# Layer 0 of a four-layer graph network: two half-height row blocks at the start, x loaded first, a wider V tile, a matmul spread of the first row terms, and the layernorm applied on GpSimd

## The chip, the cores and the metric

The kernel is one program on one core of a Trainium2 chip. The metric is the device time of one execution in microseconds, lower is better. A core has five engines with an instruction queue each, and each queue runs in order: TensorE (matmul, PE in the profile, with PEld for its weight loads), VectorE (DVE), ScalarE (ACT), GpSimd (POOL) and SyncE (SP, which here only starts DMA transfers). Transfers are also started from the ACT and POOL queues; an instruction that starts one occupies its queue until it is issued.

## What is computed

Four layers, each `x = x + layer(relu(layernorm(x)), adj)`, on x of 4096 x 256 (float32) with an adjacency matrix of 4096 x 4096 (int32, under 1% ones). Layer 0 is the one that the change works on. Of its reference, this part matters here:

```
h = relu(layernorm(x))
Wh = h @ W                                     # 4096 x 256
e = Wh @ a_src + (Wh @ a_dst).T                # one row term, one column term
e = where(e > 0, e, 0.2 * e)
attn = softmax(where(adj > 0, e, -9e15), axis=1)
h_attn = attn @ Wh                             # the attention of layer 0
...                                            # a dense part on Wh and h_attn follows, then
x = x + layernorm(gate * h_attn + ...)
```

Layer 1 averages neighbours, layer 2 is an attention of the same kind as layer 0's (slope 0.01, its own W and a), layer 3 is a dot-product attention. They use the adjacency matrix too, in the transposed and coded form that layer 0 leaves in DRAM (`codesT`).

## The kernel before

**Tiles.** N is 4096, so there are NT = 32 row tiles of 128 rows. `xs` holds all of x in SBUF. Layer 0's attention takes RB = 4 row tiles at a time: NRB = 8 blocks. Inside a block it goes over the 32 column tiles in pairs, PPB = 16 pairs for each block, 128 pairs in all.

**Attention, one pair** (class `Attention`, `run`, line 272). For a pair of column tiles VectorE makes `y` (L265, two instructions, 128x512 each: four row tiles by one column tile) from `ab_row`, the row terms of the block spread over all partitions; GpSimd subtracts the mask codes (L269, 128x1024); ScalarE takes the exponential (L295, two of 128x512); TensorE multiplies into four accumulators (L306): two column tiles by four row tiles, and each float32 matmul stands in the trace as two instructions, so 16 for a pair. The right operand is `v`, which has the 256 columns of Wh and a column of ones, from which the softmax's denominator comes. The matmuls of a pair come LAG = 3 pairs behind its `y`; `y` has 8 buffers. When a block is done, `finish0` scales the accumulators into `xs`.

**Row terms** (`reach`, line 215). Before a block can begin, its row maxima must be known: `run` is a running minimum over all 32 column tiles of code minus column term (L227 and L229, one instruction for each column tile), LEAD = 3 pairs ahead of one block. Then `run` is copied out of PSUM (L235), transposed (L238), reduced (L241), combined with the source terms in four small instructions (L242 to L246), transposed again (L248), copied (L250), written to DRAM (L251) and read back into all partitions (L253).

**Adjacency codes** (`fresh`, line 345). A unit is one row tile by 1024 columns of `adj`, 128 units in all. A GpSimd DMA loads it and casts it to bfloat16 (L351, tile `adj_t`, 8 buffers), TensorE transposes it in eight matmuls (L354) into one PSUM tile `cT`, ScalarE turns it into codes in `turned` (L358). `turned` tiles hold four row tiles by 1024 columns, and there are 8 of them. Each is also written to `codesT` (L368, 1 MB). In the main loop `ahead(n)` makes one unit for each pair, UPB + FRESH = 24 units ahead of the pair.

**Prologue** (`block0`, line 377; `run_staggered`, eight blocks of four row tiles). Each block makes three units, loads its x (L382, SP queue), takes layernorm statistics on VectorE (L121, L122), adds epsilon (L114), raises to -0.5 on GpSimd (L116), computes an offset (L131), applies scale, offset and relu on ScalarE (L133, four of 128x256), transposes on TensorE (L144, eight matmuls), copies the two results out on VectorE and ScalarE (L109, L107), multiplies by `w2` (L150, `project`; sixteen instructions of 128x258), copies the two term columns into `sd` on VectorE (L208) and the 256 columns into `v` on ScalarE (L209), and runs `reach` for two pairs. `w2` is W with two columns `W @ a_src` and `W @ a_dst` (`weights`; W and a come over the POOL queue, L181 and L188). After the eighth block `reach` is run through the rest and three pairs of the next block.

**Other loads.** The small weights of the dense part (`bcw`, `bcb`, built in lines 397 to 425) are started on the ACT queue and combined on VectorE. `identb`, the bfloat16 identity that the adjacency transposes need, is cast on VectorE (L67).

**Order.** The engines' queues are not filled in the order of the text: a scheduler at build time takes instructions as it expects them to become ready and hoists loads as far as buffers allow. Thus the casts and copies of a later part can stand ahead of earlier work in an engine's queue, and the queue then waits for them.

Of the kernel before, what the change touches and what calls it, by code (L numbers as in the profile page):

```python
# [11 lines left out]
F32 = mybir.dt.float32  # L12
# [9 lines left out]
P = 128  # L22
# [19 lines left out]
def kernel(ctx: ExitStack, tc: tile.TileContext, w: dict, out: bass.AP):  # L42
# [24 lines left out]
    nc.vector.tensor_copy(identb, ident)  # L67
# [70 lines left out]
    def transposed_block(work, pst, h, tag):  # L138

        hT = work.tile([P, KD, BW], F32, tag=tag, name=tag)  # L140
        for k in range(KD):
            ps = pst.tile([P, BW], F32, tag="tp", name="tp")
            for i in range(BT):
                nc.tensor.transpose(ps[:, ts(i, P)], h[:, i, ts(k, P)], ident)  # L144
            evac(k, hT[:, k, :], ps)
        return hT
# [12 lines left out]

    class Attention:  # L160
        def __init__(self, outer, es, tag, slope, lag, n_y, turned, finish):
            self.tag, self.slope, self.lag, self.n_y = tag, slope, lag, n_y
            self.turned, self.finish = turned, finish
            vp = outer.enter_context(tc.tile_pool(name=f"{tag}_v", bufs=1))
            self.v = vp.tile([P, NT, D + 1], F32, name="v")
            nc.gpsimd.memset(self.v[:, :, D : D + 1], 1.0)
            vp = es.enter_context(tc.tile_pool(name=f"{tag}_sd", bufs=1))
            self.sd = vp.tile([P, NT, 2], F32, name="sd")
            self.sdst = vp.tile([P, NT], F32, name="sdst")
            self.cdst = vp.tile([P, NT], F32, name="cdst")  # L170
            self.ab_d = dram.tile([NRB, 2, RB, P], F32, name=f"{tag}_ab_d")
# [4 lines left out]
            self.blocks = [{} for _ in range(NRB)]  # L176

        def weights(self, wp, work, wm, a_srcs):

            w2 = wp.tile([P, KD, D + 2], F32, name="w2")  # L180
            nc.gpsimd.dma_start(  # L181
# [4 lines left out]
            for a in a_srcs:  # L186
                n = a.shape[0]
                nc.gpsimd.dma_start(  # L188
# [11 lines left out]
            self.w2 = w2  # L200
        def project(self, b, hT, psm):

            sd = self.sd
            for i in range(BT):
                t = b * BT + i
                ps = psm.tile([P, D + 2], F32, tag="mm", name="mm")
                products(ps, lambda k: hT[:, k, ts(i, P)], lambda k: self.w2[:, k, :], KD)
                nc.vector.tensor_copy(sd[:, t, :], ps[:, D : D + 2])  # L208
                nc.scalar.copy(self.v[:, t, 0:D], ps[:, 0:D])  # L209
            at = ts(b, BT)  # L210
            nc.vector.tensor_scalar(self.sdst[:, at], sd[:, at, 1], self.slope, None, ALU.mult)
            nc.vector.tensor_scalar(
                self.cdst[:, at], sd[:, at, 1], 1.0 - self.slope, None, ALU.mult
            )

        def reach(self, n):
# [4 lines left out]
            st = self.blocks[b]  # L221
            if c == 0:
                st["run"] = self.ps_run.tile([P, RB, P], F32, tag="run", name="run")
            for j in range(c, c + 2):
                code = self.turned(b, j // QT)[:, :, j % QT, :]
                if j == 0:
                    nc.vector.tensor_scalar(st["run"], code, self.sd[:, j, 1:2], None, ALU.subtract)  # L227
                else:
                    nc.vector.scalar_tensor_tensor(  # L229
                        st["run"], code, self.sd[:, j, 1:2], st["run"], ALU.subtract, ALU.min  # L230
# [3 lines left out]
            run = self.row_p.tile([P, RB, P], F32, tag="run", name="run_sb", bufs=1)  # L234
            nc.scalar.copy(run, st["run"])  # L235
            ps = self.ps_top.tile([P, RB, P], F32, tag="top", name="top")
            for r in range(RB):
                nc.tensor.transpose(ps[:, r, :], run[:, r, :], ident)  # L238
            src = self.sd[:, ts(b, RB), 0]
            m = self.small.tile([P, RB], F32, tag="m", name="m")  # L240
# [3 lines left out]
            ab = self.small.tile([P, 2, RB], F32, tag="ab", name="ab")  # L244
            nc.vector.tensor_tensor(ab[:, 0, :], src, m, ALU.subtract)
            nc.vector.scalar_tensor_tensor(ab[:, 1, :], src, self.slope, m, ALU.mult, ALU.subtract)  # L246
            ps = self.ps_top.tile([2 * RB, P], F32, tag="top", name="abT")
            nc.tensor.transpose(ps, ab.rearrange("p v r -> p (v r)"), ident)  # L248
            abT = self.small.tile([2 * RB, P], F32, tag="abT", name="abT_sb")
            nc.scalar.copy(abT, ps)  # L250
            nc.sync.dma_start(out=self.ab_d[b].rearrange("v r i -> (v r) i"), in_=abT)  # L251
            st["ab"] = self.row_p.tile([P, 2, RB, P], F32, tag="ab", name="ab_row")
# [5 lines left out]
        def logits(self, y, b, c, mask):  # L258

            st = self.blocks[b]  # L260
            if c == 0:
                st["b"] = self.ps_b.tile([P, RB, P], F32, tag="b", name="b")
# [765 lines left out]
```

## Time and profile before

| | us |
|---|---|
| median of 3 runs | 3092.32 (3087.59 to 3093.89) |
| profiled execution, its own time | 3085.67 |
| its span, first to last instruction | 3083.9 |
| first matmul of layer 0's attention (L306) | 114.90 |
| first matmul of its second block | 180.43 |
| last matmul of its eighth block | 630.36 |
| layer 2: last matmul of layer 1 to first of its attention | 1555.13 to 1631.18 |

Over the whole span TensorE is busy 2869.8 us (93%), VectorE 1851.4 (60%), ScalarE 1271.7 (41%), GpSimd 873.3 (28%). The page's second part, in 40 equal slices of 77 us, shows where TensorE is not full: digits 5 and 7 in the first two slices, a 6 in the slice from 1234 us, a 7 in the one from 1542 us, and 9 elsewhere. The granted TensorE clock is 0.976 on average. How to read it: the share of the span is an average; the first two slices hold the prologue of layer 0 and the start of its attention, and each stage has its own limit.

### The profile page before, as it was taken

What the parts mean: (1) busy time and instruction counts of PE and PEld (TensorE: products, weight loads), DVE (VectorE), ACT (ScalarE), POOL (GpSimd) and SP (SyncE); (2) the same over time, 40 slices, a digit from 0 to 9 for tenths busy, and PEclk for the clock granted to TensorE, in tenths of its full rate; (3) what the DMA queues carried; (4) which work ended last, traced back from release to release, by engine and by line L of the source; (5) the groups of instructions that cost most, each with busy time, mean ns of one, the idle gap of its engine ahead of it and who ended that gap; (6) DMA issues with size and microseconds to landing.
All of it is one profiled execution on the core that took longest, in us unless ns stands there. A gap on an engine that the chain in (4) does not pass through costs nothing.

```text
span 3083.9 us, 34813 instructions
## 1 busy us (share of the span) xinstructions
PE 2869.8 (93%) x13344; PEld 2336.0 (76%) x13344; DVE 1851.4 (60%) x3306; ACT 1271.7 (41%) x1924; POOL 873.3 (28%) x605
## 2 busy tenths in 40 slices
PE   5799999979999999699977999999999999999999
PEld 4688888845555555588856888788888888888888
DVE  5767676324444444544479888755856656656653
ACT  5655655358888884400044443444211211211211
POOL 3556665532333233100016555661000000000000
PEclk9899999989999999899998999999999999999999
DMA  8666664054444341234322222202111111111100
GB/s 209 144 132 136 126 139 110 7 178 129 142 129 132 122 132 40 87 110 147 99 103 82 76 77 81 76 7 69 57 38 37 58 37 37 58 37 37 56 8 7
DMA packets 103127, 268.75 MB, mean 87 GB/s; under 512 B 10704, under 2 KB 24272, under 8 KB 94768
## 3 DMA queue, kind: packets, MB, share of 16 engines
q1 hardware_dynamic: 79104, 220.30, 21.4%
q0 software_dynamic: 22464, 45.51, 8.7%
q8 instruction: 104, 1.70, 0.2%
q10 hardware_dynamic: 1392, 0.72, 0.1%
q14 instruction: 63, 0.52, 0.1%
HBM read 262.22 MB, written 37.81 MB: 97 GB/s over the span
## 4 chain that ended last, share of the span: by engine, by line
PE 27%; issue 25%; DVE 3%; POOL 2%; DMA 1%; ACT 1%; POOLq 0%; DVEq 0%; ACTq 0%
PE acc L306 12%; PE acc L723 8%; PE s L150 3%; PE mm L150 2%; PE acc L960 2%; DVE run L229 1%; POOL y L269 1%; DMA turned<-codesT 1%; DVE y L265 1%; POOL pl_rs L116 1%; POOL out_dram L973 1%; DVE pl_st L121 0%; ACT y L295 0%; DVE hT L109 0%; PE tp L144 0%
## 5 line engine op out<-in xcount | busy, mean ns | idle before, releaser
L306 PE MATMUL acc<-v,y 128*128 128x257 f32 x4096 | 927.1, 385 | 42.5 <-ACT y L295 19.9
L306 PEld LDWEIGHTS acc<-v,y 128*128 128x128 f32 x4096 | 774.4, 192 | 158.1 <-ACT hp L754 22.7
L269 POOL TENSOR_TENSOR y<-y,turned 128x1024 f32<-128x1024 f32 x256 | 547.1, 2150 | 307.7 <-DVE y L265 267.5
L295 ACT ACTIVATE y<-y,sdst 128x512 f32<-128x512 f32 x512 | 342.9, 714 | 367.7 <-POOL y L269 367.5
L265 DVE SCALAR_TENSOR_TENSOR y<-ab_row,cdst,b 128x512 f32<-128x512 f32 x512 | 362.1, 743 | 180.2 <-PE acc L306 115.8
L960 PE MATMUL acc<-v,y 128*128 128x257 f32 x2048 | 454.5, 380 | 0.4 <-DVE rden L968 0.4
L150 PE MATMUL s<-qT,hT 128*128 128x256 f32 x2048 | 445.2, 379 | 0.7 <-ACT qT L908 0.7
L150 PEld LDWEIGHTS s<-qT,hT 128*128 128x128 f32 x2048 | 389.0, 190 | 54.2 <-ACT qT L908 1.4
L960 PEld LDWEIGHTS acc<-v,y 128*128 128x128 f32 x2048 | 387.1, 190 | 55.9 <-issue 0.8
L953 ACT ACTIVATE y<-y 128x1024 f32<-128x1024 f32 x128 | 132.2, 1055 | 714.3 <-DVE y L952 710.0
L229 DVE SCALAR_TENSOR_TENSOR run<-turned,sd,run 128x512 f32<-128x512 bf16 x496 | 373.4, 753 | 49.8 <-DMA turned<-codesT 28.3
L513 ACT ACTIVATE sign<-a,limits 128x1024 bf16<-128x1024 int32 x256 | 293.8, 1148 | 79.6 <-DMA a<-in_adj_dram 75.0
L973 POOL DMA_DIRECT2D out_dram<-o x32 | 17.4, 543 | 933.7 <-DVE rden L968 931.1
L723 PE MATMUL acc<-v,eq 128*128 128x512 f32 x1024 | 239.3, 395 | 0.1
L922 DVE SCALAR_TENSOR_TENSOR y<-code,s 128x512 f32<-128x512 bf16 x256 | 175.8, 687 | 100.5 <-PE s L150 100.2
L723 PEld LDWEIGHTS acc<-v,eq 128*128 128x128 f32 x1024 | 192.6, 188 | 44.9 <-DVE eq L719 0.3
L952 DVE TENSOR_TENSOR y<-y,top 128x1024 f32<-128x1024 f32 x128 | 146.2, 1216 | 43.0 <-PE top L946 43.0
L929 DVE TENSOR_TENSOR mx<-mx,y 128x512 f32<-128x512 f32 x224 | 154.8, 691 | 7.4
L358 ACT ACTIVATE turned<-cT,log_wide 128x1024 bf16<-128x1024 bf16 x128 | 141.5, 1106 | 33.5 <-PE cT L354 33.2
L719 DVE TENSOR_SCALAR eq<-code 128x4096 fp32r<-128x4096 bf16 x32 | 73.4, 2293 | 114.8 <-PE acc L723 114.8
L150 PE MATMUL mm<-hsT,w_L_gnn_W_hz 128*128 128x512 f32 x256 | 117.4, 598 | 0.6 <-DVE hsT L576 0.6
L354 PE MATMUL cT<-identb,adj_t 128*128 128x128 bf16 x1024 | 83.2, 226 | 36.4 <-DVE identb L67 18.5
(222 smaller groups left out, 2717.3 us busy)
## 6 DMA issues: line engine op xcount, KB each, us to landing
a<-in_adj_dram SPq DMA_DIRECT2D x128, 512.0 KB, 3.8
adj_t<-in_adj_dram POOLq DMA_DIRECT2D x128, 256.0 KB, 4.5
codesT<-turned SPq DMA_DIRECT2D x32, 1024.0 KB, 5.1
code<-codesT SPq DMA_DIRECT2D x128, 256.0 KB, 3.8
turned<-codesT SPq DMA_DIRECT2D x32, 1024.0 KB, 5.4
code<-codesT SPq DMA_DIRECT2D x64, 512.0 KB, 4.9
ab_row<-l_ab_d SPq DMA_DIRECT2D x16, 512.0 KB, 3.9
xs<-in_x_dram SPq DMA_DIRECT2D x8, 512.0 KB, 11.0
```

What stands on the lines that cost most here:

```text
L150: nc.tensor.matmul(out=ps, lhsT=lhsT_of(k), rhs=rhs_of(k), start=(k == 0), stop=(k == n - 1))
L229: nc.vector.scalar_tensor_tensor(st["run"], code, self.sd[:, j, 1:2], st["run"], ALU.subtract, ALU.min)
L265: nc.vector.scalar_tensor_tensor(y[:, :, k, :], st["ab"][:, 0, :, :], self.cdst[:, c + k : c + k + 1], st["b"], ALU.add, ALU.max,)
L269: nc.gpsimd.tensor_tensor(y, y, mask[:, :, c % QT : c % QT + 2, :], ALU.subtract)
L295: nc.scalar.activation(y[:, :, k, :], y[:, :, k, :], AF.Exp, bias=self.sdst[:, c + k : c + k + 1],)
L306: nc.tensor.matmul(out=accs[b][r], lhsT=y[:, r, k, :], rhs=self.v[:, c + k, :], start=(c + k == 0), stop=(c + k == NT - 1),)
L513: nc.scalar.activation(sign, a, AF.Sign, bias=limits[:, v : v + 1], accum_out=over[:, t, v, q : q + 1],)
L723: nc.tensor.matmul(out=acc, lhsT=eq[:, ts(c, P)], rhs=v1[:, c, :, :], start=(c == 0), stop=(c == NT - 1),)
L922: nc.vector.scalar_tensor_tensor(y[:, :, c : c + 2, :], st["code"][:, :, c : c + 2, :], -BIG / UNIT, ps, ALU.mult, ALU.add,)
L929: nc.vector.tensor_tensor(mx, mx, y[:, :, c : c + 2, :], ALU.max)
L952: nc.vector.tensor_tensor(part, part, top, ALU.subtract)
L960: nc.tensor.matmul(out=accs[r], lhsT=st["y"][:, r, c, :], rhs=v3[:, c, :], start=(c == 0), stop=(c == NT - 1),)
```

## The change

It has eight parts, all around the prologue of layer 0 except the second, which layer 2 shares.

1. The eight row blocks of layer 0 become nine: `cuts = [(0, 2), (2, 2), (4, 4), ...]`. The first two have two row tiles each, and share the four `turned` tiles of the first four rows. `Attention` takes the list, and every tile of a block is cut to its height.
2. `v` becomes 259 columns: ones first, then Wh, then the source and column terms. One ScalarE copy of 128x258 replaces the VectorE copy into `sd` and the ScalarE copy of 256 columns, in layers 0 and 2.
3. For block 0 the row terms don't go through DRAM: four matmuls with a selecting matrix `picks` spread them into PSUM, and ScalarE and VectorE copy them out.
4. x is loaded ahead of the block loop, blocks alternating between the SP and ACT queues; W, a_src and a_dst of layer 0 go over the ACT queue.
5. Subtraction of the mean and scaling are done on GpSimd (four of 128x256 with two operations each), and the relu goes into the copy out of the transposes, now both on ScalarE. The offset instruction is gone.
6. Units are made by need: in the prologue block b has made b + 1 units, and 1, 2, 3, 5, 7, 9, 11, 13 are loaded; eight more buffers (`first_p`) take the first eight. In the main loop `needed(n)` counts the units of the pair 24 pairs ahead.
7. The dense part's small weights are loaded on the SP queue two pairs into the last block, and combined on VectorE eight pairs into it.
8. `identb` is cast on GpSimd.

```diff
-    nc.vector.tensor_copy(identb, ident)
+    nc.gpsimd.tensor_copy(identb, ident)
...
-    def transposed_block(work, pst, h, tag):
+    def transposed_block(work, pst, h, tag, relu=False):
...
-            evac(k, hT[:, k, :], ps)
+            if relu:
+                nc.scalar.activation(hT[:, k, :], ps, AF.Relu)
+            else:
+                evac(k, hT[:, k, :], ps)
...
-            self.v = vp.tile([P, NT, D + 1], F32, name="v")
-            nc.gpsimd.memset(self.v[:, :, D : D + 1], 1.0)
+            self.v = vp.tile([P, NT, D + 3], F32, name="v")
+            nc.gpsimd.memset(self.v[:, :, 0:1], 1.0)
...
-                nc.vector.tensor_copy(sd[:, t, :], ps[:, D : D + 2])
-                nc.scalar.copy(self.v[:, t, 0:D], ps[:, 0:D])
+                nc.scalar.copy(self.v[:, b * BT + i, 1 : D + 3], ps)
...
+            if self.picks is not None and b == 0:
+                ps = self.ps_top.tile([P, 2 * n, P], F32, tag="top", name="spread")
+                for k in range(2 * n):
+                    nc.tensor.matmul(
+                        out=ps[:, k, :], lhsT=self.picks[:, k, :], rhs=abT, start=True, stop=True
+                    )
+                for v in range(2):
+                    evac(1 - v, st["ab"][:, v, :, :], ps[:, ts(v, n), :])
+                return
...
+            cuts = [(0, 2), (2, 2)] + [(t, RB) for t in range(RB, NT, RB)]
...
+            units = [
+                (at // RB, q, r % RB)
+                for at, n in cuts for q in range(NQ) for r in range(at, at + n)
+            ]
...
+            def load(up_to):
+                for b, q, r in units[len(raw) : up_to]:
+                    pool = first_p if len(raw) < FIRST else adj_p
+                    raw.append(pool.tile([P, QW], BF16, tag="adj", name="adj_t"))
+                    nc.gpsimd.dma_start(out=raw[-1], in_=adj[ts(b * RB + r, P), ts(q, QW)])
...
+            def needed(n):
+                b, c = n // PPB, n % PPB
+                if b >= len(cuts):
+                    return len(units)
+                return cuts[b][0] * NQ + cuts[b][1] * NQ * (c + 1) // PPB
...
             def ahead(n):
-                if n + UPB + FRESH < NRB * UPB:
-                    fresh(n + UPB + FRESH)
+                fresh(needed(n + PPB + FRESH))
...
+                for b in range(NB):
+                    (nc.scalar if b % 2 else nc.sync).dma_start(
+                        out=xs[:, ts(b, BT), :],
+                        in_=x[ts(b, BW), :].rearrange("(t p) d -> p t d", p=P),
+                    )
...
-                    preln(small, xb, xb)
+                    mv = small.tile([P, BT, 2], F32, tag="pl_mv", name="pl_mv")
+                    for i in range(BT):
+                        stats_of(small, xb[:, i, :], mv[:, i, :], "pl")
+                    rs = rstd_of(small, mv, BT, "pl")
+                    load(b + 1 + max(b - 2, 0))
+                    for i in range(BT):
+                        nc.gpsimd.tensor_scalar(
+                            xb[:, i, :], xb[:, i, :], mv[:, i, 0:1], rs[:, i : i + 1],
+                            ALU.subtract, ALU.mult,
+                        )
+                    fresh(b + 1)
                     yield
-                    hT = transposed_block(work, pst, xb, "hT")
+                    hT = transposed_block(work, pst, xb, "hT", relu=True)
                     yield
                     att.project(b, hT, psm)
                     yield
-                    for n in range(2 * b, 2 * b + 2 if b < NB - 1 else PPB + LEAD):
+                    for n in range(2 * b, 2 * b + 2):
                         att.reach(n)
 
                 run_staggered([block0(b) for b in range(NB)], 2)
...
+                fresh(needed(PPB + FRESH - 1))
+                for n in range(PPB, PPB + LEAD):
+                    att.reach(n)
```

## The prediction, made before the changed kernel ran

> **What bounds the kernel now.** I read the page's slices first, then busy time by stage (microseconds from the start, then busy time and count of each engine, granted clock, DMA share, GB/s):
>
> ```profile
> 0.00:48.00 48.00, 17.65 (x96) 13.95 (x97) 23.23 (x114) 16.83 (x28) 18.14 (x37) 1.00 0.81 200
> 48.00:90.00 42.00, 36.62 (x297) 31.46 (x297) 27.64 (x73) 39.67 (x72) 11.25 (x20) 1.00 1.03 223
> 90.00:115.00 25.00, 8.48 (x70) 6.90 (x69) 18.18 (x30) 9.78 (x12) 7.32 (x10) 0.53 0.97 248
> 115.00:181.00 66.00, 64.50 (x351) 55.18 (x351) 49.68 (x83) 40.91 (x58) 50.17 (x32) 0.97 0.39 81
> 181.00:581.00 400.00, 387.35 (x2264) 333.09 (x2264) 270.36 (x439) 229.08 (x314) 248.68 (x176) 1.00 0.53 117
> ```
>
> From 115 us on TensorE is full; what happens there before moves everything behind it. Ahead of it three stages differ: a start with TensorE idle for 30 of 48 us; projections, where ScalarE is the full one (39.67 of 42); and 25 us in which nearly all waits. The waits up to 115 us name the first stage:
>
> ```profile
> PE cT L354 <- DVE identb L67: 18.5, 1, 18.5
> ACT xs L133 <- DVE pl_off L131: 18.8, 2, 17.9
> DVE bcb L414 <- DMA b_row<-in_L_gnn_b_bcdt_dram: 6.4, 1, 6.4
> ```
>
> VectorE's queue stood behind a weight of the dense part and behind late x; the identity cast and the first offset were behind these. The timeline of the third stage:
>
> ```profile
> 88.12 0.61 PE L354 MATMUL cT<-identb,adj_t 128*128 128x128 bf16 x8
> ...
> 96.04 0.24 ACT L250 COPY abT_sb<-abT 8x128 f32<-8x128 f32 x1
> ...
> 96.58 0.34 SPq L251 DMA_DIRECT2D l_ab_d<-abT_sb  x1
> 103.44 0.34 SPq L253 DMA_DIRECT2D ab_row<-l_ab_d  x1
> ...
> 109.72 0.59 ACT L263 COPY b<-ab_row 128x512 f32<-128x512 f32 x1 [4.72 <-DMA ab_row<-l_ab_d]
> ...
> 114.90 3.37 PE L306 MATMUL acc<-v,y 128*128 128x257 f32 x7 [8.84 <-ACT y L295]
> ```
>
> Projections end at 88.3; 8.0 us of small steps, 13.4 us of DRAM (96.3 to 109.7), 5.2 us until TensorE has an exponential. Last, the steady pair and the groups that price the new work:
>
> ```profile
> 141.77 0.61 PE L354 MATMUL cT<-identb,adj_t 128*128 128x128 bf16 x8
> 142.22 3.69 PE L306 MATMUL acc<-v,y 128*128 128x257 f32 x16
> 145.74 0.61 PE L354 MATMUL cT<-identb,adj_t 128*128 128x128 bf16 x8
> ...
> L592 POOL TENSOR_SCALAR sz<-sz,b_L_gnn_D 128x512 f32<-128x512 f32 x32 | 50.0, 1564 | 109.0 <-ACT sz L589 108.2
> L116 POOL TENSOR_TENSOR pl_rs<-pl_ve,mhalf 128x4 f32<-128x4 f32 x32 | 33.6, 1049 | 111.5 <-DVE pl_ve L114 91.8 <-DVE sd L208 9.7 <-ACT hT L107 2.5
> L133 ACT ACTIVATE xs<-xs,pl_off,pl_rs 128x256 f32<-128x256 f32 x19 | 11.8, 642 | 0.0
> L358 ACT ACTIVATE turned<-cT,log_wide 128x1024 bf16<-128x1024 bf16 x20 | 22.8, 1140 | 0.6 <-PE cT L354 0.5
> ```
>
> A pair takes 3.97 us: 16 instructions in 3.52 us from start to start (0.22 each) and a unit's transposes in 0.45.
>
> **What the Trainium skill says.** "GPSIMD Engine Reference", Elementwise — side-by-side cycle accounting: about 2.6 cycles of 1.2 GHz an element for two inputs, 1.03 for light one-input bodies. The mask subtraction (1024 elements in 2.13 us, 2.5 cycles) agrees; L592, one input and one operation, took 3.05 ns an element, 3.7 cycles, so I use the trace. "TensorE: Matmul & The Clock Gate", What's actually happening: an idle array drops to half clock. The trace agrees: 0.53 granted between 90 and 115, and eight adjacency transposes took 1.01 us there against 0.61. "DMA: Bandwidth & Descriptors", Issuing engines are not separate DMA queues: two queues save only issue time. No run here separates that; I give the second x queue no bandwidth.
>
> **The change, part by part.** The target is when TensorE begins the rows from tile 4 on: 180.43 before. Both kernels have the same work and a similar lead in units from there.
>
> *Start.* The first x rows were in SBUF at 5.1, and W now leads its queue. Statistics to 7.4 (four times 0.52, and epsilon), power 1.05, four GpSimd scalings: 12.0. Transposes and a copy out: projection at 14.5, against 34.74. The VectorE traffic jam is gone with parts 7 and 8; x loads that precede adj now hold up nothing, since a block needs 0.5 MB each 5.6 us (0.09 MB/us against 200 GB/s moved).
>
> *The scalings* are the unknown: 128x256, two operations. From L592 by size 0.78 us; double if the second operation costs a pass of its own, 1.56; from below 0.22 by the page's 1.03 cycles. I take 0.85, as the generic loop seems to dominate one operation already. GpSimd for each block: 4 x 0.85 + 1.05 + 1.6 unit loads at 0.56 = 5.35 us. TensorE: 16 x 0.22, 8 x 0.12, one unit at 0.45, 5.0 us. ScalarE: two copies at 0.6, four at 0.39, one unit at 1.14: 3.9 us, where before 4 x 0.64 + 3 x 1.14 + 0.6 + 4 x 0.39 = 8.1 was the bound. VectorE: 2.2 of statistics, four half-height running minima at about 0.42 (0.75 halved plus a fixed part), 0.2: 4.1 us. I take 5.6 a block. The first, at half clock, ends at 21.5 (sixteen at about 0.46, as at 34.74); seven more end at 60.7, against 88.3.
>
> *End of the prologue.* The small steps stay 8.0 us. Four spread matmuls about 1.0 (priced by L248, 0.42 cold, overlapping), copies 0.7, then the copy of b, y, subtraction, exponential at half size: 3.0. First attention matmul at 73.4; say 73, against 114.90. The DRAM trip, 13.4 us, is what part 3 takes out.
>
> *Half-height blocks.* Each pair has 8 matmul instructions, 1.76 us, plus 12 units over block 0's 16 pairs (0.33 each) and 16 over block 1's (0.45): 2.1 and 2.2. Per pair VectorE needs 4 x 0.42 = 1.7 us in block 0 and 2.2 in block 1 (full-height minima for block 2); GpSimd 1.08 + 0.56; ScalarE 0.9 + 0.8 to 1.1. All are near TensorE's time, and `cT` has one buffer, so I take 2.3 and 2.4: 37 + 38 us. The two block changes: at a change before, the terms were ready 13 us after L238, and TensorE had seven pairs left, 28 us; seven half pairs are 16 us, so with y, subtraction and exponential behind (3 us) they are even or late: 3.5 us each, 7 in all. Second-half start: 73 + 37 + 38 + 7 = 155. Gain 25.
>
> *Without cost.* Part 7's eight VectorE instructions (about 2 us) and seven SP issues lie in the last block, where VectorE is busy two thirds; if uncovered, 2 us. The 259-column rows change no length. Part 2 in layer 2: VectorE is busy 9.4 and 8.9 of the 10 us from 1580 and from 1590, and gives 32 small copies up there, 0.07 to 0.16 us each with waits for matmuls: gain 2 us, between 0 and 5, and ready-times slip by the longer ScalarE copy at most 0.3 each.
>
> Sum: 3085.67 - 25 - 2 = 3058.7 for the profiled execution. The median lies 6.65 above it, so the forecast is 3092.3 - 27 = 3065.
>
> **Rivals.**
> - *GpSimd bounds the prologue.* At 1.56 a scaling, a block takes 8.2 us; seven cost 18 us more, plus 3 on the first: gain 6, with layer 2: 3086. For: L592 is far above the page's rate, and power alone takes 1 us for four numbers. Against: that instruction has no second input and one pass. Chance 0.13.
> - *Everything fits.* Scaling near 0.5, pairs at the TensorE rate (2.1 and 2.2), no boundary stall: 70 + 34 + 35 + 1 = 140; gain 40 + 3: 3049. Chance 0.17.
> - *Slower: hand-offs bound the half blocks.* A half pair still passes VectorE, GpSimd, ScalarE and TensorE in order, unit loads wait on GpSimd's queue for transposes (up to 5.1 us here) with subtractions behind them. With 73 and 7 as above it decides at (180.4 - 80) / 32 = 3.1 us a pair; at 3.4 it gives 189, 8.4 us later; less 2 in layer 2: 3099. Against: GpSimd paced full pairs at 2.1 us between 112 and 137, without TensorE starving. Chance 0.10.
>
> **Numbers.** My case has 0.60 and by its unknowns (scaling 0.5 to 1.2, pairs 2.15 to 2.7) reaches 3053 to 3079. Down to 3047 and up to 3087 takes in most of the fast case and half of the GpSimd one. Within 0.2%, 6 us, is about what a measurement cannot tell from no change: faster means below 3086. Faster 0.60 + 0.17 + 0.06 = 0.83; same 0.08; slower 0.09.
>
> **What would show it.** Right: first projection near 15 us, first attention matmul between 70 and 80, rows of tile 4 near 155, no DRAM step before block 0. Wrong: GpSimd full between 15 and 80 with TensorE waiting for scaled x; pairs of 3 us in the first two blocks; or a start near 155 given back before 630 - 25 us, where layer 0's attention should end.

## The result and the profile after

The changed kernel takes 3092.19 us (median of 12 runs, 3086.83 to 3099.19), the kernel before 3094.74 in the same series: ratio 0.9995, interval 0.9982 to 1.0007, no change that can be told. The forecast was 3065. The profiled execution took 3090.16 us (span 3088.4), against 3085.67 (3083.9) before.

| microseconds from the start | before | predicted | after |
|---|---|---|---|
| first projection matmul (L153) | 34.74 | 14.5 | 25.39 |
| last projection over | 88.3 | 60.7 | 74.3 |
| first attention matmul (L321) | 114.90 | 73 | 84.69 |
| first matmul of block 1 | (no such block) | 113.5 | 126.54 |
| first matmul of the rows from tile 4 | 180.43 | 155 | 178.27 |
| attention of layer 0 over | 631.0 | 605 | 631.9 |

The start did become 30 us earlier. Of these, 2.2 were left when the rows of tile 4 began, and none at the end of layer 0. The busy times of the changed kernel by stretches of 20 us (stretch, length, then busy time and count of TensorE, its weight loads, VectorE, ScalarE and GpSimd, granted clock, DMA share, GB/s):

```profile
0.00:20.00 20.00, 0.95 (x2) 0.36 (x2) 8.82 (x46) 0.00 (x0) 6.64 (x19) 1.00 0.92 274
20.00:40.00 20.00, 17.55 (x97) 14.65 (x98) 6.53 (x31) 12.10 (x21) 19.85 (x19) 1.00 0.30 42
40.00:60.00 20.00, 17.04 (x99) 13.70 (x98) 12.35 (x39) 10.12 (x22) 19.90 (x22) 1.00 0.46 68
...
80.00:100.00 20.00, 17.31 (x109) 14.20 (x109) 19.42 (x50) 15.17 (x25) 13.71 (x16) 0.83 1.01 275
...
140.00:160.00 20.00, 19.47 (x136) 15.97 (x135) 15.67 (x32) 16.45 (x27) 13.96 (x17) 1.00 0.97 210
160.00:180.00 20.00, 10.56 (x78) 8.83 (x77) 14.43 (x25) 10.54 (x14) 8.32 (x10) 0.72 0.86 213
```

Three readings. In the first 20 us no engine is full, only the transfers (0.92). From 20 to 60 GpSimd is: 19.85 and 19.90 of 20. From 160 to 180 TensorE works 10.56 us, and the transfers are at 0.86 there, after 80 us near 1. The timeline of the same kernel (start, duration, engine, line, operation, tiles; in brackets the idle time before and what ended it) shows each:

```profile
7.90 0.43 DVE L201 CUSTOM_DVE_ANT_0 junk<-w,a 128x256 f32<-128x256 f32 x1 [7.90 <-DMA a<-in_L_gnn_a_src_dram]
...
8.25 0.42 DVE L121 BATCH_NORM_STATS2 pl_st<-xs 128x6 f32<-128x256 f32 x1
11.70 0.43 DVE L201 CUSTOM_DVE_ANT_0 junk<-w,a 128x256 f32<-128x256 f32 x1 [3.02 <-DMA a<-in_L_gnn_a_dst_dram]
...
15.02 0.15 DVE L114 TENSOR_SCALAR pl_ve<-pl_mv 128x4 f32<-128x4 f32 x1
...
17.02 4.83 POOL L490 TENSOR_SCALAR xs<-xs,pl_mv,pl_rs 128x256 f32<-128x256 f32 x4
...
22.12 1.28 ACT L401 ACT_TABLE_LOAD   x1 [22.12 <-PE cT L395]
...
24.43 1.07 ACT L146 ACTIVATE hT<-tp 128x512 f32<-128x512 f32 x2
...
152.54 0.66 PE L242 MATMUL top<-ident,run_sb 128*128 128x128 f32 x4 [0.31 <-ACT run_sb L239]
...
157.64 0.24 ACT L254 COPY abT_sb<-abT 8x128 f32<-8x128 f32 x1
...
157.91 0.28 SPq L266 DMA_DIRECT2D l_ab_d<-abT_sb  x1
162.99 1.95 PE L321 MATMUL acc<-v,y 128*128 128x257 f32 x8
163.83 0.32 SPq L267 DMA_DIRECT2D ab_row<-l_ab_d  x1
...
171.36 0.59 ACT L277 COPY b<-ab_row 128x512 f32<-128x512 f32 x1 [4.82 <-DMA ab_row<-l_ab_d]
172.03 5.36 DVE L279 SCALAR_TENSOR_TENSOR y<-ab_row,cdst,b 128x512 f32<-128x512 f32 x8 [4.82 <-ACT b L277]
174.35 0.53 POOL L386 DMA_DIRECT2D adj_t<-in_adj_dram  x1 [6.32 <-PE cT L395]
174.89 4.22 POOL L283 TENSOR_TENSOR y<-y,turned 128x1024 f32<-128x1024 f32 x2
177.31 1.32 ACT L310 ACTIVATE y<-y,sdst 128x512 f32<-128x512 f32 x2
178.27 4.16 PE L321 MATMUL acc<-v,y 128*128 128x257 f32 x9
```

VectorE's first instruction was a product of W and a, which waited for `a_src` until 7.90 (in the kernel before, block 0's statistics began at 5.10). It made one statistic of block 0 at 8.25 and then stood 3.02 us for `a_dst`, because the other products were next in its queue; block 0's epsilon came at 15.02 (7.4 predicted). The scalings ended at 21.85, and ScalarE then loaded a table and evacuated an adjacency unit before it rectified block 0. Before tile 4, a and b left for DRAM at 157.91, the read could be issued 5.92 us later and landed another 7.5 us later; TensorE had run out of half-height pairs at 164.94. After b was there (171.95), it took another 6.3 us to the first matmul: GpSimd's subtraction stood behind an adjacency load that waited for a transpose until 174.35.

The scaling's price, in the groups of instructions of the changed kernel (count, busy us, mean ns, idle before):

```profile
L490 POOL TENSOR_SCALAR xs<-xs,pl_mv,pl_rs 128x256 f32<-128x256 f32 x32 | 38.7, 1214 | 0.3
```

### The profile page after: what moved, and what is told of

Read it like the earlier page. It is cut to its first block, busy times and chain, and to the rows that moved or that the text cites. A ratio compares the mean times of both kernels' runs of the same rounds, so it can differ in the third digit from the quotient of the medians.

```text
span 3088.4 us, 34938 instructions
## 1 busy us (share of the span) xinstructions
PE 2880.1 (93%) x13353; PEld 2342.5 (76%) x13353; DVE 1850.6 (60%) x3296; ACT 1269.3 (41%) x1936; POOL 913.4 (30%) x651
## 5 line engine op out<-in xcount | busy, mean ns | idle before, releaser
L321 PE MATMUL acc<-v,y 128*128 128x257 f32 x4096 | 932.1, 386 | 35.1 <-ACT hp L836 17.3
L321 PEld LDWEIGHTS acc<-v,y 128*128 128x128 f32 x4096 | 775.8, 192 | 147.9 <-ACT hp L836 22.1
L283 POOL TENSOR_TENSOR y<-y,turned 128x1024 f32<-128x1024 f32 (+1 forms) x272 | 550.1, 2037 | 293.1 <-DVE y L279 245.2
L310 ACT ACTIVATE y<-y,sdst 128x512 f32<-128x512 f32 (+1 forms) x544 | 351.0, 689 | 361.6 <-POOL y L283 361.2
L279 DVE SCALAR_TENSOR_TENSOR y<-ab_row,cdst,b 128x512 f32<-128x512 f32 (+1 forms) x544 | 368.4, 711 | 169.1 <-PE acc L321 110.5
L153 PE MATMUL s<-qT,hT 128*128 128x256 f32 x2048 | 445.2, 380 | 0.7 <-ACT qT L991 0.7
L153 PEld LDWEIGHTS s<-qT,hT 128*128 128x128 f32 x2048 | 389.9, 190 | 53.2 <-ACT qT L991 1.4
L233 DVE SCALAR_TENSOR_TENSOR run<-turned,v,run 128x512 f32<-128x512 bf16 (+1 forms) x527 | 380.5, 722 | 60.8 <-DMA turned<-codesT 27.1
L799 DVE TENSOR_SCALAR eq<-code 128x4096 fp32r<-128x4096 bf16 x32 | 73.4, 2294 | 115.8 <-PE acc L803 115.8
L153 PE MATMUL mm<-hsT,w_L_gnn_W_hz 128*128 128x512 f32 x256 | 117.9, 600 | 0.1
L153 PE MATMUL mm<-w_L_gnn_g_w,comb 128*128 128x512 f32 x256 | 113.5, 593 | 0.0
```

Source lines behind the costliest of these rows:

```text
L153: nc.tensor.matmul(out=ps, lhsT=lhsT_of(k), rhs=rhs_of(k), start=(k == 0), stop=(k == n - 1))
L233: nc.vector.scalar_tensor_tensor(st["run"], code, dst, st["run"], ALU.subtract, ALU.min)
L279: nc.vector.scalar_tensor_tensor(y[:, :, k, :], st["ab"][:, 0, :, :], self.cdst[:, c + k : c + k + 1], st["b"], ALU.add, ALU.max,)
L283: nc.gpsimd.tensor_tensor(y, y, mask[:, :, c % QT : c % QT + 2, :], ALU.subtract)
L310: nc.scalar.activation(y[:, :, k, :], y[:, :, k, :], AF.Exp, bias=self.sdst[:, c + k : c + k + 1],)
L321: nc.tensor.matmul(out=acc, lhsT=y[:, r, k, :], rhs=self.v[:, c + k, 0 : D + 1], start=(c + k == 0), stop=(c + k == NT - 1),)
```

## The experiments

All are edits of the changed kernel. Positions are from one profiled execution each (us); the rows of tile 4 begin with the 257th instruction of the attention's matmuls (two half-height blocks have 256, and so has one full block). Ratios are to the kernel before, on the same chip. A comparison between runs of different batches is by these ratios.

| run | batch | first projection | first attention matmul | rows of tile 4 | layer 0's attention over | ratio, interval |
|---|---|---|---|---|---|---|
| changed kernel | | 25.39 | 84.69 | 178.27 | 631.9 | 0.9995, 0.9982 to 1.0007 |
| e1_spread3 | 1 | 25.09 | 85.67 | 167.65 | 624.7 | 0.9964, 0.9948 to 0.9981 |
| e2_ln_act | 1 | 23.94 | 78.79 | 173.20 | 627.2 | 0.9981, 0.997 to 0.9993 |
| e3_a_first | 1 | 25.16 | 85.18 | 178.73 | 633.4 | 1.0, 0.999 to 1.0009 |
| e4_full | 1 | 25.16 | 98.56 | 171.19 | 626.5 | 0.9968, 0.9954 to 0.9981 |
| e5_x_first | 2 | 23.02 | 84.59 | 165.50 | 623.2 | 0.9958, 0.9945 to 0.9972 |
| e6_lead5 | 2 | 26.49 | 87.04 | 169.45 | 629.9 | 0.9977, 0.9969 to 0.9986 |
| e7_xf_act_lead5 | 2 | 20.56 | 78.32 | 161.14 | 621.6 | 0.9934, 0.9914 to 0.9953 |
| e8_xf_half_lead5 | 2 | 20.95 | 85.89 | 168.17 | 628.9 | 0.9973, 0.9964 to 0.9982 |
| e9_forced | 3 | 23.79 | 83.65 | 165.20 | 623.1 | 0.9959, 0.9944 to 0.9974 |
| e10_forced_act | 3 | 21.43 | 77.37 | 159.11 | 617.3 | 0.9926, 0.9911 to 0.9941 |
| e11_p7 | 3 | 25.98 | 87.26 | 168.41 | 624.8 | 0.9951, 0.9934 to 0.9969 |
| e12_order | 4 | 15.89 | 88.13 | 170.03 | 627.1 | 0.997, 0.9956 to 0.9984 |

### The DRAM trip before tile 4: e1_spread3

```diff
-            if self.picks is not None and b == 0:
+            if self.picks is not None and b < 3:
-                ps = self.ps_top.tile([P, 2 * n, P], F32, tag="top", name="spread")
...
                 for v in range(2):
+                    ps = self.ps_top.tile([P, n, P], F32, tag="top", name="spread")
+                    for k in range(n):
...
```

The spread goes in two halves, so that eight rows fit the same PSUM tile.

> The changed kernel, with the row terms of blocks 0, 1 and 2 all spread by TensorE, so that no DRAM trip stands before the rows of tile 4. Theory A (the DRAM trips at the two early block changes give back some of the head start): the first matmul for the rows of tile 4 comes 8 to 12 us earlier than the 178.3 us of the changed kernel, near 168, and layer 0's attention ends 6 to 12 us earlier than 631.8. Rival B (the row maxima themselves are late at that change, because the half-height pairs run as fast as VectorE and ScalarE can follow): the DRAM trip is hidden by that, the first matmul moves by under 3 us.

Theory A came: the rows of tile 4 begin at 167.65, 10.6 us earlier. Layer 0 ends 7.2 us earlier than in the changed kernel, and the ratio says 0.36% faster than before. The timeline at the change to tile 4:

```profile
155.82 0.26 ACT L254 COPY abT_sb<-abT 8x128 f32<-8x128 f32 x1 [0.24 <-PE abT L252]
...
156.37 1.15 PE L261 MATMUL spread<-abT_sb,picks 8*128 8x128 f32 x8
...
159.04 1.15 PE L261 MATMUL spread<-abT_sb,picks 8*128 8x128 f32 x8
...
161.80 0.59 ACT L278 COPY b<-ab_row 128x512 f32<-128x512 f32 x1
...
167.65 2.00 PE L322 MATMUL acc<-v,y 128*128 128x257 f32 x8 [0.20 <-ACT y L311]
...
171.34 0.61 PE L396 MATMUL cT<-identb,adj_t 128*128 128x128 bf16 x8 [1.68 <-ACT turned L402]
171.78 4.55 PE L322 MATMUL acc<-v,y 128*128 128x257 f32 x20
```

From the copy of a and b to their use it is 6.0 us, against 13.7 through DRAM. Between the last half-height matmul and the first of tile 4 lie 0.6 us instead of 13.3; the longest idle stretch of TensorE around it, 1.7 us, comes half a pair later. From the first attention matmul to tile 4 it takes 82.0 us instead of 93.6. The transfers were as full as in the changed kernel (0.96 and 0.95 during block 1's matmuls), so the stall was the trip and not a lack of adjacency. The DMA page of the Trainium skill ("DMA: Bandwidth & Descriptors", Latency and other measured facts) gives the access to DRAM 0.2 us on average and 2 us under high load. No run here times one access; for the 4 KB store plus its broadcast read these runs measured 5.1 to 7.9 us in the steady blocks and 13.7 where the transfers were full.

### GpSimd's scaling: e2_ln_act

```diff
-                        nc.gpsimd.tensor_scalar(
-                            xb[:, i, :], xb[:, i, :], mv[:, i, 0:1], rs[:, i : i + 1],
-                            ALU.subtract, ALU.mult,
+                        nc.scalar.activation(
+                            xb[:, i, :], xb[:, i, :], AF.Relu,
+                            scale=rs[:, i : i + 1], bias=off[:, i : i + 1],
```

> The changed kernel with part 5 alone undone: scale, offset and relu of the first layernorm on ScalarE again, GpSimd has only the power and the loads. Theory A (four GpSimd scalings of 1.21 us, 4.83 us a block, pace the prologue at 7.0 us a block): projections come every 5.5 to 6 us, the last ends near 64 instead of 74.2 and the first attention matmul stands near 74 instead of 84.7; the later end of layer 0's attention shows less than this, because the wait at the change to the rows of tile 4 takes part of it. Rival C (ScalarE becomes the bound as in the kernel before, 2.6 us of scaling more in a block): projections every 7 us and no gain.

With the offset on VectorE and the relu on ScalarE as in the kernel before, the first attention matmul comes 5.9 us earlier (10.7 forecast), the projections come 5.1 to 5.9 us apart from the second to the last, and layer 0 ends 4.7 us earlier. The stall before tile 4 stays (159.81 to 173.20). So the price of part 5 is some 5 us. Rival C did not come: ScalarE is not the bound here.

### Full-height blocks: e4_full

```diff
-            cuts = [(0, 2), (2, 2)] + [(t, RB) for t in range(RB, NT, RB)]
+            cuts = [(t, RB) for t in range(0, NT, RB)]
```

with block 0 spread by TensorE, as in e1, and units loaded for whole blocks.

> The changed kernel with part 1 undone: eight blocks of four row tiles, block 0's terms still spread by TensorE, units made four for each two prologue blocks. Theory A (the half blocks lose at the change to tile 4 what they win at the start): the first attention matmul comes 5 to 8 us later than 84.7, since four more running minima and eight more units stand before it, but there is no stall of 13 us at 165; layer 0's attention ends between 618 and 630, at least 2 us earlier than the 631.8 of the changed kernel. Rival E (the half blocks are what lets TensorE start early and are worth their cost): it ends later than 632.

Attention starts 13.9 us later than in the changed kernel (5 to 8 forecast), its second block follows the first after 0.9 us, and layer 0 still ends 5.4 us earlier, as in e1 within 2 us. The half-height blocks gain a start and pay it back: two of them need 82.0 us in e1, for rows that take a full block 72.6 us in e4 and 65.5 in the kernel before.

### Why the first projection was late: e3_a_first, e5_x_first, e9_forced, e12_order

In e3 the loads of `a_src` and `a_dst` go first on SP, ahead of x:

```diff
-                eng.dma_start(
+                (nc.sync if eng is nc.scalar else eng).dma_start(
                     out=a2[:, at : at + n],
```

> The changed kernel with a_src and a_dst loaded first on the SP queue, W first on the ACT queue, x behind them. Theory A (VectorE's queue holds the first statistics behind the products of W with a, which wait for a_dst until 11.7 us): the first projection comes 3 to 5 us earlier than 25.4, but the GpSimd-paced blocks behind it move by the same 3 to 5 us and the first attention matmul stands near 80. Rival D (the first x rows are what is late, as all eight x loads share the engines): the a rows come early, the first projection does not move by more than 1 us.

The products were over at 8.5, and the first projection did not move: VectorE now waited for x until 12.54.

```profile
12.54 0.75 DVE L121 BATCH_NORM_STATS2 pl_st<-xs 128x6 f32<-128x256 f32 x2 [4.00 <-DMA xs<-in_x_dram]
```

I first read this as "x itself is late". It isn't so simple: the edit had put x behind the two vectors in SP's queue. For the next two runs that order is turned round: x leads SP's queue with all eight loads, and ScalarE's queue keeps W and a alone. In e5 the products stand after block 0's statistics in the program; in e9 they must follow them, since each first takes a copy of the deviation:

```diff
-                    (nc.scalar if b % 2 else nc.sync).dma_start(
+                    nc.sync.dma_start(
...
+                    if after is not None:
+                        nc.vector.tensor_copy(junk[:, 0:BT], after)
                     nc.vector.tensor_tensor_reduce(
                         junk, w2[:, k, 0:D], a2[:, ts(v, D)], 1.0, 0.0, ALU.mult, ALU.add,
```

> On top of the version that spreads three blocks: all eight loads of x go on SP, W and the two a vectors alone on ScalarE's queue, and VectorE forms W times a after the statistics of block 0 instead of before. Theory A (the first projection is late because block 0's statistics stand in VectorE's queue behind the products that wait for a_dst, and x block 0 shares the transfers with x block 1): the statistics of block 0 are over by 7, the first projection starts at 17 (15 to 19) instead of 25.1, GpSimd keeps its 6 to 7 us a block, the first attention matmul comes at 76 to 77 instead of 85.7, the time falls by 8 to 9 us to about 3071. Rival F (the prologue's transfers are the bound, so that the order only moves the wait): the first projection moves by less than 3 us, or the later blocks' x is late by as much; first attention matmul 83 or later, time 3077 to 3080.

In e5 the scheduler hoisted the products again, and block 0's epsilon, at 12.16, still stood behind `a_dst` (1.75 us of waiting). Against e1 the first projection moved by 2.1 us and the attention began at 84.59. Those are rival F's positions, but not for its reason: block 0's statistics ran from 8.04 without a wait for x.

> On top of the version that spreads three blocks: x on SP alone, and the products of W and a now can't go before the statistics of block 0 on VectorE, since each first takes a copy of block 0's reciprocal deviation into its scratch tile (four copies of 128x4 are added). In the run before, which only moved them in the program, they still stood in front of the last steps of block 0, and the first projection came at 23.0. Theory A (block 0's statistics wait behind a_dst in VectorE's queue, not for x): statistics over by 8, the first projection at 16 to 18, the first attention matmul at 77 to 80 with GpSimd at the same 6 to 7 us a block, ratio 0.993 to 0.995. Rival F (x itself arrives too late): the statistics wait for xs until 10 or later, first projection at 21 or later, ratio 0.996.

The timeline of e9:

```profile
5.28 0.75 DVE L121 BATCH_NORM_STATS2 pl_st<-xs 128x6 f32<-128x256 f32 x2 [5.28 <-DMA xs<-in_x_dram]
...
9.88 0.43 DVE L121 BATCH_NORM_STATS2 pl_st<-xs 128x6 f32<-128x256 f32 x1 [2.84 <-DMA xs<-in_x_dram]
10.22 0.15 DVE L114 TENSOR_SCALAR pl_ve<-pl_mv 128x4 f32<-128x4 f32 x1
...
10.53 1.04 POOL L116 TENSOR_TENSOR pl_rs<-pl_ve,mhalf 128x4 f32<-128x4 f32 x1 [7.90 <-DVE pl_ve L114]
13.32 1.01 POOL L116 TENSOR_TENSOR pl_rs<-pl_ve,mhalf 128x4 f32<-128x4 f32 x1 [1.74 <-DVE pl_ve L114]
14.29 0.62 POOL L392 DMA_DIRECT2D adj_t<-in_adj_dram  x1
14.96 10.12 POOL L498 TENSOR_SCALAR xs<-xs,pl_mv,pl_rs 128x256 f32<-128x256 f32 x8
...
20.52 1.28 ACT L407 ACT_TABLE_LOAD   x1 [20.52 <-PE cT L401]
...
23.79 4.62 PE L153 MATMUL mm<-w,hT 128*128 128x258 f32 x10
```

x is there at 5.28 and the statistics are over by 7.0: theory A of this run, up to there. Then the rest of its forecast fails, and rival F's projection and ratio come, though block 0's x was in time. Three queues one after another explain it. Block 0's epsilon stands behind a statistic of block 1, which waits for x (2.84 us); its scalings stand behind block 1's power and an adjacency load (from 11.6 to 14.96); its rectification behind the table load and an adjacency unit (1.2 us after its transposes, which end at 21.64). The Trainium skill ("Perfetto Trace Analysis", Tensor Engine Instruction) calls the queues of ScalarE, VectorE and GpSimd strictly first in, first out; this trace agrees: in each of the three, block 0's next step was ready, for 2.8, 3.4 and 1.2 us, while the queue stood at another's.

e12 forces the order for block 0, on top of e10 (below):

```diff
+                x_in(0)
+                warm = small.tile([P, 1], F32, tag="warm", name="warm")
+                nc.scalar.activation(warm, log_wide, AF.Exp)
...
                     if b == 0:
+                        nc.gpsimd.tensor_copy(xs[:, BT, 0:1], rs[:, 0:1])
+                        for later in range(1, NB):
+                            x_in(later)
                         att.columns(work, rs)
```

> The version before it (x first on SP, ScalarE scales, three blocks spread) with the orders of block 0 forced: x block 1's load waits for a copy of block 0's reciprocal deviation, so nothing of block 1 can stand ahead of block 0 on VectorE or GpSimd, and a first exponential of a small tile loads ScalarE's table at the start. Theory Q (what is left of the late first projection, 21.4 here and 25.4 in the changed kernel, is instructions of later blocks ahead of block 0 in in-order queues, and the table load): block 0's epsilon at 7, its power from 7.2 to 8.3, the first projection at 13 to 15, the first attention matmul at 69 to 72, layer 0 ends at 610 to 614, ratio 0.989 to 0.992. Rival R (later blocks need the early transfers as much as block 0, and x block 1 onwards is now late behind adjacency loads): first projection at 13 to 15 but the last one still at 61 or later, first attention matmul at 76 or later, ratio 0.992 to 0.994.

Theory Q nearly held for block 0: epsilon at 7.28, first projection at 15.89 (13 to 15 forecast). That is 1.4 us from the prediction's, but with the four scalings on ScalarE, in 2.07 us. Order and table load were changed together, so their shares are not separated. For the rest rival R held, harder than it was set, and in part through the edit itself. Only block 1's load waits for the copy, so the scheduler put x of five later blocks ahead of it: SP had issued six loads of x by 8.2 us, waited 1.5 us, and issued block 1's as the seventh at 9.76. And it filled GpSimd's queue with eight adjacency loads at that time.

```profile
9.66 3.71 POOL L392 DMA_DIRECT2D adj_t<-in_adj_dram  x7
...
30.56 0.75 DVE L121 BATCH_NORM_STATS2 pl_st<-xs 128x6 f32<-128x256 f32 x2 [16.03 <-DMA xs<-in_x_dram]
```

The first attention matmul came at 88.13, 10.8 us later than with the loads in their old order (e10). The DMA page of the skill ("DMA: Bandwidth & Descriptors", Queues, rings and completion order) says that an engine takes turns between the queues that have work, packet by packet. The trace agrees: from 16 to 28 us SP's queue moved 1011 packets (1.00 MB) and GpSimd's 1018 (1.86 MB). So block 1's x waited for the five blocks ahead of it, and the adjacency loads took every second packet meanwhile; e12 does not separate the two.

### The layer's later loss: e6_lead5, e11_p7

From the row maxima of the rows from tile 8 on (217.85 us in before) to the end of layer 0 the changed kernel lost 4.4 us of its lead, and e1, e2, e4, e9, e10 and e12 lost 4.7 to 7.4, in loops that are the same. All but 0.3 us of the 4.4 is TensorE standing still: in this stretch it is busy 401.65 us in before and 401.97 in the changed kernel, and idle 11.5 and 15.6. e6 starts the row terms five pairs ahead (`LEAD = 5` in layer 0), so that the DRAM trips have more time; e11 puts the loads of the dense part's weights back where they were. Both build on e1.

```diff
-    LEAD = 3
+    LEAD = 5
```

> On top of the version that spreads three blocks: in layer 0 a block's row terms are begun five pairs ahead of its attention instead of three, so that the trip of a and b through DRAM has some 21 us instead of 12.6. Theory G (the 3 us that layer 0 loses against before between 415 and 490 us are TensorE standing still because the trip of one block shares the transfers with adjacency loads): TensorE's idle time behind xs and turned at that block change falls from 3.2 us to under 1, layer 0 ends 3 to 4 us earlier than with three pairs, time about 3076. Rival H (the loss comes from the order in ScalarE's queue or from the schedule of the adjacency units, not from the trip): the idle time stays at 3 us, the time within 1 us of 3079.4.

At the three changes from 270 to 445 us TensorE's waits behind `xs` and `turned` fell from 2.1, 1.8 and 3.2 us (e1) to 0.9, 0.9 and 1.5, in part as G says. But a wait for `ab`, VectorE's small steps, rose from 0.65 to 1.4 at each change, the attention began 1.4 us later, and layer 0 ended 5.2 us later than in e1. The ratio is worse than e1's (0.9977 against 0.9964): neither theory's time came.

```diff
-                last = n - (len(cuts) - 1) * PPB
-                if last == 2:
...
+                bcdt = w["L0_gnn_W_bcdt"].rearrange("(k p) m -> p k m", p=P)
+                for at, part in ((0, 0), (S, 2 * S)):
+                    nc.scalar.dma_start(
...
```

> The version that spreads three blocks with the dense part's weights loaded as before: on ScalarE's queue in tiles of the prologue, their VectorE products behind the prologue, no tiles taken from the adjacency pool. Theory K (the 1.2 to 1.5 us that layer 0's stretch before its last block has lost against before come from tiles of the adjacency pool that these loads take): the second wait on turned in that stretch (0.83 us near 521) goes, the stretch takes 64 instead of 65.3 us. Theory L (prologue jam, the price of what is undone): these loads share the transfers with x, and the first attention matmul comes 2 to 6 us later than 85.7. Total ratio 0.997 to 0.998 if both hold, 0.996 if neither.

The second wait on `turned` (0.83 us) is gone, the stretch takes 64.6 instead of 65.3 us, as K says, and the attention begins 1.6 us later (L: 2 to 6). Both are small; the total can't be told from e1's.

The traces tie part of the loss to the length of the trip. For the two changes between blocks from 270 to 365 us, from the copy of a and b to the copy of b, and TensorE's idle time in the 32 us that begin 2 us ahead of the first copy:

| kernel | trip, idle | trip, idle |
|---|---|---|
| before | 5.8, 1.9 | 6.8, 2.7 |
| changed | 6.8, 2.7 | 5.7, 1.8 |
| e1 | 6.7, 2.7 | 6.5, 2.5 |
| e10 | 6.7, 2.6 | 6.8, 3.0 |
| e11 | 7.2, 3.2 | 6.6, 2.6 |

At the next change the trip took 5.4 us before and 6.9 to 7.6 in the others, with 1.5 and 3.9 to 4.6 us idle. Here the trips of 6.5 us and more go with a second wait of TensorE on `turned`, those of 5.4 to 5.8 us with one. This is a correlation; the change near 415 us alone accounts for 2.4 to 3.1 us of the loss. Why the trips came out longer there, and the rest of the loss, stay open: no run changed the trip alone.

### All causes together: e7_xf_act_lead5, e8_xf_half_lead5, e10_forced_act

e7 is e5 with the edits of e2 and e6; e10 is e9 with the edit of e2, so with three pairs of lead. e8 is e7 with half of the tiles on GpSimd:

```diff
                     for i in range(BT):
+                        if i % 2:
+                            nc.gpsimd.tensor_scalar(
+                                xb[:, i, :], xb[:, i, :], mv[:, i, 0:1], rs[:, i : i + 1],
+                                ALU.subtract, ALU.mult,
+                            )
+                            continue
                         nc.scalar.activation(
```

> The two edits before together (x first on SP and the products behind the statistics; five pairs of lead), and the layernorm's scale, offset and relu of layer 0 back on ScalarE. If theories A and G hold and their gains add to the 6 us that ScalarE's layernorm gave the first attention matmul: first projection 15 to 17, first attention matmul 69 to 71, layer 0 ends 17 to 20 us earlier than in the changed kernel, time 3063 to 3068. Rival (with GpSimd out of the way the adjacency loads bound layer 0's first 180 us, so that an earlier start only waits for them): first attention matmul 70, but layer 0 ends less than 10 us earlier than in the changed kernel, time 3073 or more.

> As the run before it, but each block's four layernorm tiles are shared out, two on ScalarE and two on GpSimd, and the transposed block is still rectified on ScalarE. If the scaling of four tiles in a row is the chain of the prologue: first projection 1 to 2 us earlier than with ScalarE alone, first attention matmul 67 to 70, time 3061 to 3067. Rival (another engine or the transfers of x pace the blocks by then): within 1 us of the run before it.

> The same with the layernorm of layer 0 on ScalarE instead of GpSimd, three pairs of lead. If each cause is what the runs so far say (first projection by VectorE's queue, the pace of the projections by GpSimd, the stall before tile 4 by the DRAM trip): first projection 15 to 17, first attention matmul 72 to 75, layer 0 ends at 614 to 618, ratio 0.991 to 0.993. Rival (TensorE, 18.4 us busy in each 20 us of the prologue once ScalarE scales, or the adjacency loads take over as the bound): first attention matmul 77 or later, layer 0 ends after 619, ratio 0.994 or more.

e7 missed its 69 to 71 by 7 us and its 3063 to 3068 by 8, and e8 began its attention 7.6 us later than e7: between 20 and 70 us ScalarE waited 9.9 us for the offset, and the offset 15.6 us for GpSimd's power, which shares GpSimd's queue with the scalings and the adjacency loads. e10 is the fastest version: 3069.78 against 3093.09, 0.74% faster than before (0.59 to 0.89%), which beats both kernels. Its rival was right on the start (77.37, TensorE the bound of the prologue), its theory on the total. Against e9, on the same chip, part 5 alone is worth 9.9 us of median; the profiles show 5.8 of it at the end of layer 0, and no run explains the rest, which lies where the code is the same. The busy times of e10:

```profile
20.00:40.00 20.00, 18.19 (x96) 15.19 (x97) 13.14 (x58) 16.64 (x35) 9.92 (x15) 1.00 0.96 180
40.00:60.00 20.00, 18.76 (x116) 16.17 (x117) 10.23 (x25) 15.41 (x34) 0.00 (x0) 1.00 0.00 1
60.00:80.00 20.00, 14.61 (x94) 11.88 (x93) 15.56 (x42) 13.14 (x22) 7.13 (x10) 0.77 0.58 137
```

TensorE is at 18.2 and 18.8 of 20 in the projections, and GpSimd and the transfers stand idle from 40 to 60: all 16 adjacency buffers are full, and the next load, at 66.31, waited 29.2 us for a transpose.

## Why the prediction was wrong

At tile 4 it was 23.3 us too early (155 against 178.27): 10.9 at the start, 2.7 in the pace of the projections, -2.3 at the end of the prologue, 1.4 and 0.4 in the half-height blocks, 9.8 at the change to tile 4, and 0.4 from writing 73 for 73.4. By its own steps:

- **Start, 10.9 us: failed.** "A start with TensorE idle" was read rightly, and that parts 7 and 8 clear VectorE of the identity cast and the dense weights as well. The sentence "the VectorE traffic jam is gone" was wrong: the products of W and a, and in e9 statistics of the next block, took their place ahead of block 0. Block 0 was 7.6 us late at epsilon, 9.9 at the end of the scalings (21.85 against 12.0), 10.9 at the projection. The transfers do not forbid the predicted time: e12 reached 15.89, with the scalings on ScalarE; on GpSimd it would be 18.7, an estimate (15.89 - 2.07 + 4.83). I also left out ScalarE's table load (1.28 us) and the unit that it evacuates first (1.1), of which 1.2 us show behind the transposes.
- **The scalings, mis-sized.** 0.85 us taken, 1.214 measured, inside the bounds 0.22 and 1.56. With it, and the adjacency loads on the same queue, GpSimd needs 6.5 to 7.0 us a block instead of 5.35 (5.6 taken for a block) and bounds the prologue, as the first rival said, at a lower price than its 1.56. From the first projection to the end of the last only 2.7 us of it show, since the first one was late for other reasons and the next ones caught up; e2 prices the whole part at 5.9 us of start.
- **End of the prologue: right.** 10.4 us from the last projection to the first attention matmul against 12.7; the trip that part 3 takes out is out.
- **Half-height blocks: right.** 41.9 us for block 0 with its change against 40.5, and 38.4 us for block 1's own matmuls against 38.
- **The change to tile 4, 9.8 us: failed in size, in all three of its terms.** 3.5 us forecast, 13.3 measured. "Ready 13 us after L238" came from a change with the transfers at 0.68 (150 to 163 us in before); here it was 19.4 us (152.54 to 171.95) with the transfers at 0.99 (150 to 172). The prediction had a trip through full transfers in its own lines, 13.4 us at 0.97, and did not use it here. TensorE had not seven half pairs left but five, 12.4 us of work instead of 16. And y, subtraction and exponential took 6.3 us instead of 3; the kernel before, in the prediction's own lines, took 5.2 there (109.72 to 114.90). 19.4 + 6.3 - 12.4 makes the 13.3. e1 shows that without the trip the stall is gone, e4 that without half-height blocks it does not come up.
- **"The same work and a similar lead from there": failed by 3.1 us,** between tile 4 and the end of layer 0. From the row maxima of tile 8 on it is idle time of TensorE, in part beside longer trips; the cause stays open.
- **Part 7 without cost: right** within what can be told (e11). **Layer 2: 2 us forecast,** 3.2 measured: its prologue takes 72.87 instead of 76.05 us.

The late start, the mis-sized scaling, the change to tile 4 and the later idle time use up the gain (a slip in the sum, 21.5 where 14.5 and sixteen at 0.46 make 21.9, is too small to matter); the slower-than-before rival, pairs of 3.1 us or more, was not what happened. The profiled execution of the changed kernel is even 4.5 us longer than that of before, although layer 0 ends only 0.9 later and layer 2 gains 3.2: between layer 0's attention and layer 2's first projection, where the code is the same but for the width of V, before took 938.1 us and the others 938.4 to 950.2, the changed kernel 946.6. Single profiles with this same code differ by 12 us there, and the one of before was a low one (3085.67, with medians of 3091.6 to 3095.5 in the series here). So this difference is not shown to be an effect of the change, and the medians agree with the rest of the account (0.9 - 3.2 = -2.3, measured -2.55).

## What to carry to other kernels

A step that becomes ready early only starts early if nothing waits ahead of it in its engine's queue: when a load is moved forward, list for every engine on the chain what the scheduler puts in front, because removing one blocker uncovers the next. Price a small trip through DRAM by the traffic of the stage it will run in, not by the quiet stage where it was seen, and shrink no block to a size whose remaining work is shorter than that trip and the steps behind it. An engine that looks free takes work only at its own price: GpSimd needed 1.21 us for what ScalarE does in 0.60.

## What the runs showed that I had not expected

- GpSimd's scaling with two per-partition scalars takes 1.214 us for 256 elements a partition, 4.7 ns an element, dearer than the one-operation form's 3.05. The forecast's guess that a second operation costs little was wrong; what of the difference is the operation and what the form of the scalars, no run separates.
- The eight 128x128 spreads with 8 rows contracted, 16 instructions, took TensorE 2.30 us, and the whole way through PSUM 6.0, against 13.7 through DRAM with the transfers full.
- An order forced at one place moved the scheduler's loads at another: a wait on one block's load let five later blocks pass it in the same queue, and e12 gained 5.5 us at the first projection and lost 10.8 at the first attention matmul.
